# Division of attention by its sums: transposes and VectorE against factors sent through DRAM, with other places for the router's steps and for half of the last norms

## The chip, the cores and the metric

The kernel runs on one core of one Trainium2 chip, in one launch. The metric is the device time of that core in microseconds (us). Most of it is the span that the profile covers; the small rest lies around the span.

## The reference, cut to what matters

Two layers run over x of 8 x 256 tokens with 256 features. The first layer is an attention by correlation and a mixture of eight experts with balanced assignment; its output is added to x. The second layer is an ordinary cross attention with 16 heads of 16 features, and a mixture with one shared and eight routed experts, two of them for each token. The change is in the second layer:

```python
def _L1_xattn_ref(x, data, Wq, bq, Wkv, bkv, Wp, bp):
    q = (x @ Wq + bq).reshape(bs, n_ctx, HEADS, d)
    kv = (data @ Wkv + bkv).reshape(bs, n_data, HEADS, 2 * d)
    k, v = (kv[..., :d], kv[..., d:])
    scores = jnp.einsum('bqhd,bkhd->bhqk', q, k) * scale
    attn = jax.nn.softmax(scores, axis=-1)
    out = jnp.einsum('bhqk,bkhd->bqhd', attn, v).reshape(bs, n_ctx, WIDTH)
    return out @ Wp + bp

def _L1_ffn_ref(hidden_states, gate_W, w1_e, w3_e, w2_e, w1_s, w3_s, w2_s):
    probs = jax.nn.softmax(flat @ gate_W.T, axis=-1)
    top_v, top_i = jax.lax.top_k(probs, 2)
    # gates: top_v at top_i, zero elsewhere
    # routed: sum over e of gates * (silu(x w1_e) * (x w3_e)) w2_e
    # shared: mean over n of (silu(x w1_s) * (x w3_s)) w2_s
    return 0.5 * shared + 0.5 * routed

x = x + _L1_xattn_ref(_layernorm(x), ctx_1024, ...)
x = x + _L1_ffn_ref(_layernorm(x), ...)
```

The softmax of the attention is computed as exponentials, products with the values, and a division by the sum of the exponentials at the end. That division is what the change is about.

## The kernel before, in words

All work is in float32. The order of instructions on each engine is the order of the program's text: the scheduler is set to manual. The tokens of x lie in X, 128 per row of the tile, 16 such rows; a batch b is two of them (TPB = 2, S = 256).

**The attention loop.** Before it, keys KT and values VA of all batches are there, but for two last pieces of VA (`vals`). VA has 32 columns per head (HW): 16 features, and a column of ones that makes the product of exponentials and values carry the sum of the exponentials as its row 16 (DH). The loop runs over b = 0 to 7 and over c = 0, 1, a half of the heads, so 16 half batches. For each, `scores(b, c, kt)` is called with kt = 0 and 1, for each half of the keys: four matmuls (32 rows by 512 columns, L2652; the trace records each as two), each into its own PSUM buffer of ps_s (four buffers of 512 floats per partition), and four exponentials on ScalarE (L2660). Between and after the two calls stand pieces of other work: `values(prev, 0)` and `values(prev, 1)` of the half batch before (L2667), `keep` (L2677), which copies the product pv from its single PSUM buffer to ov, `queries` (L2619 and its copies QM at L2626 on ScalarE and L2633 on VectorE), `turn_q` (transposes of the normalised x for the queries, L2605), `add_y` (the first layer's output is added, loaded as yg from DRAM) and `batch_stats` for batches to come.

**The division.** For a batch whose two half batches are kept, `turn_back` transposes ov with eight matmuls against the identity (L2687), so that tokens are on the partitions; then VectorE takes reciprocals of the 16 sums (L2694) and multiplies (L2695) into `on`. `turn_out` transposes `on` back with four matmuls (L2706), VectorE copies to oT (L2712), and `project_out` multiplies by wp (L2718) and adds to X (L2726).

**The router and the mixture's rows.** `batch_stats(b, "m")` and `norm_m(b)` give the normalised rows HP; both halves of `norm_m` run on GpSimd (L2581). `turn_m` transposes them into HT (L2605, copy L2608 on ScalarE). `route(g)` is a generator of eight steps for four token rows, i.e. two batches: logits (L2797), a transpose (L2808), softmax and top two on VectorE, a cumulative count (L2850, L2851), and row numbers `to`. Each finished router puts eight sends in a list; `send(n)` issues the next n: indirect DMAs from GpSimd that write rows of HP to the table Td in DRAM (L2892). Each send waits for the one before it to land.

**After the loop.** The last values and norms, the routers 2 and 3 and the remaining sends are interleaved with `classic_up`, the shared expert's up projection for the first 512 tokens (L3196, eight steps, two PSUM buffers of ps_s for each); `first_down` is its down projection (L3439). Then come ten further blocks of 512 rows with a Strassen scheme (L3234, L3293). The first block of routed rows reads Td (R, L3491) and transposes R (L3509). The weights of the shared expert are loaded in five DMAs at the end of the half batch (0, 0).

**Queues.** Direct DMAs are issued from SP in program order, and an issue that waits holds all behind it.

The loop's centre:

```python
scores(b, c, 0)
if prev:
    values(*prev, 0)
send()
...          # c == 0: project_out(b - 2); c == 1: turn_back(b - 1), turn_m(b - 2)
scores(b, c, 1)
...          # c == 0: batch_stats(b - 2, "m"), norm_m(b - 2)
send()
if prev:
    values(*prev, 1)
    keep(*prev)
...          # c == 0: queries(b + 1, ...); c == 1: turn_out(b - 1), turn_q(b + 2)
```

Of the kernel before, what the change touches and what calls it, by code (L numbers as in the profile page):

```python
# [9 lines left out]
F32 = mybir.dt.float32  # L10
# [9 lines left out]
P = 128  # L20
# [1066 lines left out]
def fast_path(  # L1087
# [170 lines left out]
    B32 = p0.tile([P, 32], F32, name="B32")  # L1258
    miss = p0.tile([P, 2], F32, name="miss")
# [1270 lines left out]
    ps_s = banks.enter_context(tc.tile_pool(name="ps_s", bufs=4, space=PSUM))  # L2530
# [47 lines left out]
    def batch_norm(b, tag, dst, engs):  # L2578
        mv, r1 = norms.pop((tag, b))
        for j, eng in enumerate(engs):  # L2580
            eng.tensor_scalar(  # L2581
                dst[:, j, :],
                X[:, TPB * b + j, :],
                mv[:, j, 0:1],
                r1[:, j : j + 1],
                ALU.subtract,
                ALU.mult,
            )
# [54 lines left out]
    ex, pvs, ovs, ons, oTs = {}, {}, {}, {}, {}  # L2643

    def scores(b, c, kt):
# [3 lines left out]
        ps = [ps_s.tile([P, 2, S], F32, tag="p", name=f"p{g}") for g in range(4)]  # L2649
        for g in range(4):  # L2650
            rows = slice(32 * g, 32 * g + 32)
            nc.tensor.matmul(  # L2652
                ps[g].rearrange("p m q -> p (m q)"),
                KT[rows, c, k0 : k0 + P],
                QM[b][rows, c].rearrange("p m q -> p (m q)"),
                start=True,
                stop=True,
            )
        for g in range(4):
            nc.scalar.activation(e4[:, g], ps[g], AF.Exp, scale=scale)  # L2660
# [13 lines left out]

    def keep(b, c):
        ovs[b, c] = pxs.tile([P, 2, S], F32, tag="ov", name="ov", bufs=3)
        nc.vector.tensor_copy(ovs[b, c], pvs.pop((b, c)))  # L2677

    def turn_back(b):

        on = pxs.tile([P, TPB, NB, 2, 4, DH], F32, tag="on", name="on")
        ons[b] = on
        for qt in range(TPB):
            pt = ps_m.tile([P, NB, 2, 4, HW], F32, tag="pm", name="pt")
            for c in range(NB):
                for m in range(2):
                    nc.tensor.transpose(  # L2687
                        pt[:, c, m].rearrange("p g w -> p (g w)"),
                        ovs[b, c][:, m, qt * P : (qt + 1) * P],
                        ident,  # L2690
                    )
            pv = pt.rearrange("p c m g w -> p (c m g) w")
            rs = small.tile([P, H, 1], F32, tag="rs", name="rs")
            nc.vector.reciprocal(rs, pv[:, :, DH : DH + 1])  # L2694
            nc.vector.tensor_tensor(  # L2695
                on[:, qt].rearrange("p c m g d -> p (c m g) d"),
                pv[:, :, 0:DH],
                rs.to_broadcast([P, H, DH]),
                ALU.mult,
            )  # L2700

    def turn_out(b):
        pt = ps_m.tile([P, NB, TPB, P], F32, tag="pm", name="pt")
        for c in range(NB):
            for qt in range(TPB):
                nc.tensor.transpose(  # L2706
                    pt[:, c, qt, :],
                    ons[b][:, qt, c].rearrange("p m g d -> p (m g d)"),
                    ident,
                )  # L2710
        oTs[b] = pxs.tile([P, NB, TPB, P], F32, tag="oT", name="oT")
        nc.vector.tensor_copy(oTs[b], pt)  # L2712

    def project_out(b):
        pp = ps_m.tile([P, TPB, D], F32, tag="pm", name="pp")
        for qt in range(TPB):
            for c in range(NB):
                nc.tensor.matmul(  # L2718
                    pp[:, qt, :],
                    oTs[b][:, c, qt, :],  # L2720
# [10 lines left out]
    def norm_m(b):  # L2731
        batch_norm(b, "m", HP[:, TPB * b : TPB * (b + 1), 0:D], (nc.gpsimd,) * TPB)
# [169 lines left out]

    def load_up(pool, e):
# [60 lines left out]
    gates = None  # L2964
    prev = None
    for b in range(B):
        for c in range(NB):
            scores(b, c, 0)
            if (b, c) == (3, 0):
                router_weights()  # L2970
            if prev:
                values(*prev, 0)
            send()
            if gates:
                next(gates, None)
            if prev is None:
                list(vals(4, 1, ps_m, nc.vector.tensor_copy))
            elif b == 0:
                turn_q(1)
                norm_q(2, nc.vector, nc.vector)  # L2980
                queries(1, 0)
                queries(1, 1)
            elif c == 0:
                if b >= 2:
                    project_out(b - 2)
            else:
                if b >= 1:
                    turn_back(b - 1)
                if b >= 2:
                    turn_m(b - 2)  # L2990
                if 2 < b + 2 < B:
                    norm_q(b + 2, nc.vector, nc.vector if b < 2 else nc.gpsimd)
                    add_bias(b + 2)
            scores(b, c, 1)
            if gates:
                next(gates, None)
            if c == 0 and b >= 2:
                batch_stats(b - 2, "m")
                norm_m(b - 2)
            send()  # L3000
            if prev:
                values(*prev, 1)
                keep(*prev)
            if gates:
                next(gates, None)
            if c == 0:
                if 0 < b and b + 1 < B:
                    queries(b + 1, 0)
                    queries(b + 1, 1)
                if b + 2 < B and b:  # L3010
                    add_y(b + 2)
                    batch_stats(b + 2, "q")
                if b >= 4 and b % 2 == 0:
                    gates = route(b // 2 - 2)
                    next(gates)
            else:
                if b >= 1:
                    turn_out(b - 1)
                else:
                    add_bias(2)  # L3020
                if b + 2 < B:
                    turn_q(b + 2)
            if prev is None:
# [27 lines left out]
                WS = load_l1(wsp, -1)  # L3051
            if (b, c) == (1, 0):
                router_columns()
            prev = b, c
# [129 lines left out]
    def classic_up(wab, xs, acts):  # L3184

        for k in range(NK):
            act = act_tile()
            acts.append(act)
            for h in range(2):
                f = h * NK + k  # L3190
                fs = slice(f * P, (f + 1) * P)
                pgt = ps_s.tile([P, TB], F32, tag="p", name="pgt")
                pu = ps_s.tile([P, TB], F32, tag="p", name="pu")
                for m, ps in enumerate((pgt, pu)):
                    for kc in range(KC):
                        nc.tensor.matmul(  # L3196
                            ps,
# [7 lines left out]
                nc.scalar.activation(a, two(pgt), AF.Silu)  # L3205
                nc.vector.tensor_tensor(a, a, two(pu), ALU.mult)
# [245 lines left out]
    def first_down(wc, acts, between):  # L3452

        pys = [ps_s.tile([P, D], F32, tag="p", name="py") for _ in range(FULL)]

        for q in (0, 1):
            whole_down(pys[q], wc, acts, q, range(NK - 1))
        between()
        for q in range(FULL):
            whole_down(pys[q], wc, acts, q, range(NK - 1, NK) if q < 2 else range(NK))  # L3460
            add_whole(pys[q], q)
            if q % 2:
                nc.sync.dma_start(out=odv[:, q - 1 : q + 1, :], in_=X[:, q - 1 : q + 1, :])
# [208 lines left out]
    def run_all(*gens):  # L3672
        for gen in gens:
            for _ in gen:
                pass


    values(*prev, 0)
    project_out(B - 2)
    values(*prev, 1)  # L3680
    keep(*prev)
# [228 lines left out]
```

## Time and profile before

| | us |
|---|---|
| median of three runs | 831.42 (829.79 to 832.22) |
| the profiled execution, whole | 830.43 |
| its span | 828.7 |
| TensorE busy in the span | 806.3 |
| first score matmul of the attention loop | 223.0 |
| first matmul of the shared expert's down projection (L3439) | 381.1 |
| GpSimd's last send (L2892) starts | 427.1 |
| SP issues R (L3491) | 429.7 |
| first transposes of R (L3509) | 452.5 |

Times in the lower rows count from the start of the span. Granted TensorE clock: 0.998 of full. Durations of matmuls overlap: the profile gives a matmul the time from its start to its modelled end, while the next has begun. So the cost of a piece of TensorE work is read from the start of it to the start of what follows.

### The profile page before, as it was taken

What the parts mean: (1) busy time and instruction counts of PE and PEld (TensorE: products, weight loads), DVE (VectorE), ACT (ScalarE), POOL (GpSimd) and SP (SyncE); (2) the same over time, 40 slices, a digit from 0 to 9 for tenths busy, and PEclk for the clock granted to TensorE, in tenths of its full rate; (3) what the DMA queues carried; (4) which work ended last, traced back from release to release, by engine and by line L of the source; (5) the groups of instructions that cost most, each with busy time, mean ns of one, the idle gap of its engine ahead of it and who ended that gap; (6) DMA issues with size and microseconds to landing.
All of it is one profiled execution on the core that took longest, in us unless ns stands there. A gap on an engine that the chain in (4) does not pass through costs nothing.

```text
span 828.7 us, 13872 instructions
## 1 busy us (share of the span) xinstructions
PE 806.3 (97%) x5188; PEld 636.2 (77%) x5188; DVE 522.3 (63%) x1470; ACT 348.7 (42%) x720; POOL 216.8 (26%) x293
## 2 busy tenths in 40 slices
PE   7999999999999999999999999999999999999997
PEld 6546787778745555557898989797979798999996
DVE  6377877440456586555775866767676758586731
ACT  4344454324377777431333233333333433443430
POOL 6251131230125455452330000202111232112020
PEclk9999999999999999999999999999999999999999
DMA  8395567942160000042120474656575754311023
GB/s 261 97 277 177 178 207 224 297 158 84 51 178 15 14 1 28 34 168 89 67 67 26 142 242 135 190 168 187 172 199 161 201 167 122 105 13 20 8 35 124
DMA packets 87316, 105.40 MB, mean 127 GB/s; under 512 B 9000, under 2 KB 77832, under 8 KB 87208
## 3 DMA queue, kind: packets, MB, share of 16 engines
q1 hardware_dynamic: 78568, 91.10, 35.0%
q0 software_dynamic: 7920, 13.02, 7.2%
q8 instruction: 43, 0.70, 0.4%
q10 hardware_dynamic: 752, 0.30, 0.1%
q14 instruction: 33, 0.27, 0.1%
HBM read 80.61 MB, written 25.37 MB: 128 GB/s over the span
## 4 chain that ended last, share of the span: by engine, by line
PE 88%; DMA 5%; DVE 3%; POOL 2%; ACT 1%; issue 1%; ACTq 0%; SPq 0%; DVEq 0%; POOLq 0%
PE a L3234 18%; PE e L3234 9%; PE a L3293 9%; PE py L2389 6%; PE ph L2372 5%; PE B L3234 5%; PE e L3293 4%; PE p L2652 4%; PE py L3439 3%; PE pv L2667 3%; PE B L3293 2%; PE pp L2718 2%; DMA R<-NMd,ids 2%; PE pgt L3196 2%; PE pp L2619 2%; PE pu L3196 2%
## 5 line engine op out<-in xcount | busy, mean ns | idle before, releaser
L3518 POOL DMA_INDIRECT Od<-Y,ids x32 | 51.6, 1612 | 300.5 <-DVE T L3083 184.0
L3222 ACT COPY B<-a 128x512 f32<-128x512 f32 (+1 forms) x54 | 28.6, 531 | 180.5 <-PE a L3234 142.6
L2660 ACT ACTIVATE ex<-p,scale 128x512 f32<-128x512 f32 x128 | 77.2, 689 | 27.5 <-PE p L2652 26.3
L3234 PE MATMUL a<-T,HP 128*128 128x256 f32 x288 | 73.9, 379 | 0.0
L3083 DVE TENSOR_TENSOR cc<-e,s 128x512 f32<-128x512 f32 x44 | 30.4, 691 | 58.0 <-PE e L3234 58.0
L3234 PE MATMUL a<-RT,wab 128*128 128x256 f32 x256 | 66.6, 383 | 0.0
L3083 DVE TENSOR_TENSOR act<-act 128x256 f32<-128x256 f32 (+1 forms) x120 | 61.4, 512 | 2.7
L2372 PE MATMUL ph<-RT,w 128*128 128x256 f32 x256 | 61.7, 389 | 0.8 <-ACT RT L2359 0.7
L2389 PE MATMUL py<-w,A 128*128 128x256 f32 x256 | 61.6, 388 | 0.0
L3234 PEld LDWEIGHTS a<-T,HP 128*128 128x128 f32 x288 | 54.0, 190 | 7.0
L3234 PEld LDWEIGHTS a<-RT,wab 128*128 128x128 f32 x256 | 46.4, 190 | 8.4 <-issue 1.6
L2381 ACT ACTIVATE A<-ph,b1c 128x256 f32<-128x256 f32 x64 | 30.0, 472 | 53.9 <-PE ph L2372 50.6
L2372 PEld LDWEIGHTS ph<-RT,w 128*128 128x128 f32 x256 | 45.3, 190 | 8.9 <-ACT A L2381 1.1
L2389 PEld LDWEIGHTS py<-w,A 128*128 128x128 f32 x256 | 46.6, 190 | 6.4
L2892 POOL DMA_INDIRECT Td<-HP,to x32 | 32.9, 1030 | 56.9 <-DMA Td<-HP,to 51.6
L2652 PE MATMUL p<-QM,KT 32*128 32x512 f32 x256 | 43.4, 640 | 0.4 <-DVE QM L2633 0.4
L3083 DVE TENSOR_TENSOR act<-act,cc 128x512 f32<-128x512 f32 x44 | 30.4, 691 | 17.6 <-ACT act L3268 17.1
L2399 POOL DMA_INDIRECT Yd<-Y,ids x16 | 15.7, 984 | 81.9 <-DVE Y L2398 49.0
L2667 PE MATMUL pv<-ex,VA 128*32 128x256 f32 x512 | 34.5, 385 | 0.2 <-DVE ov L2677 0.2
L3249 ACT COPY s<-a 128x512 f32<-128x512 f32 x44 | 25.7, 585 | 20.4 <-PE a L3234 20.4
L2667 PEld LDWEIGHTS pv<-ex,VA 128*32 128x32 f32 x512 | 13.5, 109 | 27.0 <-issue 11.7
L3234 PE MATMUL e<-T,wab 128*128 128x256 f32 x128 | 33.0, 380 | 0.3 <-DVE T L3083 0.3
(525 smaller groups left out, 1745.0 us busy)
## 6 DMA issues: line engine op xcount, KB each, us to landing
w<-in_L_ffn_w_dram SPq DMA_DIRECT2D x16, 1024.0 KB, 6.0
wab<-in_L_ffn_w_e_dram SPq DMA_DIRECT2D x16, 1024.0 KB, 4.9
wc<-in_L_ffn_w_e_dram SPq DMA_DIRECT2D x8, 1024.0 KB, 5.4
sab<-in_L_ffn_w_e_dram SPq DMA_DIRECT2D x32, 256.0 KB, 2.9
R<-Td SPq DMA_DIRECT2D x8, 530.0 KB, 3.7
sc<-in_L_ffn_w_e_dram SPq DMA_DIRECT2D x16, 256.0 KB, 2.8
Td<-blank SPq DMA_DIRECT2D x2, 1590.0 KB, 10.2
X<-in_x_dram SPq DMA_DIRECT2D x4, 512.0 KB, 5.3
```

Source lines behind the costliest of these rows:

```text
L2372: nc.tensor.matmul(ph, w1[:, kc, f * P : (f + 1) * P], RT[:, kc, :], start=(kc == 0), stop=(kc == KC - 1),)
L2381: nc.scalar.activation(A[:, f, :], ph, AF.Gelu_apprx_tanh, bias=b1c[:, e, f : f + 1])
L2389: nc.tensor.matmul(py, A[:, f, r * P : (r + 1) * P], w2[:, f, :], start=(f == 0), stop=(f == NF - 1),)
L2652: nc.tensor.matmul(ps[g].rearrange("p m q -> p (m q)"), KT[rows, c, k0 : k0 + P], QM[b][rows, c].rearrange("p m q -> p (m q)"), start=True ...
L2660: nc.scalar.activation(e4[:, g], ps[g], AF.Exp, scale=scale)
L2667: nc.tensor.matmul(pvs[b, c][32 * g : 32 * g + 32, m, :], VA[:, b * TPB + kt, 8 * c + 2 * g + m, :], ex[b, c, kt][:, g, m, :], start=(kt = ...
L2892: nc.gpsimd.indirect_dma_start(out=Td, out_offset=bass.IndirectOffsetOnAxis(ap=to[g][:, k, j : j + 1], axis=0), in_=HP[:, GT * g + j, :], ...
L3083: eng.tensor_tensor(out, a, b, op)
L3196: nc.tensor.matmul(ps, wab[:, m, kc, fs], xs[kc], start=(kc == 0), stop=(kc == KC - 1),)
L3234: nc.tensor.matmul(ps[:, m * HT2 : (m + 1) * HT2], self.w.get(m, left, self.k), self.x.part[right], start=start and m == 0, stop=True, ski ...
L3293: nc.tensor.matmul(ps[:, qs], self.acts[k][:, left, qs], self.w.get(right, k), start=start and i == 0 and k == 0, stop=(k == NK - 1), skip ...
L3518: nc.gpsimd.indirect_dma_start(out=Od, out_offset=bass.IndirectOffsetOnAxis(ap=ids, axis=0), in_=Y, in_offset=None, compute_op=ALU.add,)
```

## The change

In `scores`, ps_s has two buffers of 1024 floats in place of four of 512, two of the four matmuls write to each, and an exponential covers one such buffer. `turn_back` and `turn_out` are gone. `keep` now sends the sums from ov to a tile rs of 128 x 16 and ov itself to DRAM (VD). `factors`, one half batch later, takes reciprocals of rs on VectorE, writes them to DRAM (FD), loads the 16 feature rows of each head from VD (num) and each head's factors from FD, repeated over 16 partitions (fac). `scaled_values`, another half batch later, multiplies both on GpSimd into oT. In the loop, both halves of `values` and `keep` stand between the two calls of `scores`; `queries` and `turn_m` (of b - 3 in place of b - 2) follow the second call at c = 0, `turn_q` and `project_out` at c = 1. `norm_m` has one row on GpSimd and one on VectorE, apart in time. Routers 0 and 1 start at (4, 1) and (6, 1) in place of (4, 0) and (6, 0), and their steps stand at other places. The shared weights come in six DMAs, one per half batch. After the loop, the same pieces stand in another order; the sends of routers 1 and 2 that are left wait for router 2 to finish. `classic_up` and `first_down` use the larger PSUM buffers, and `first_down` adds and stores its results in pairs.

```diff
-    ps_s = banks.enter_context(tc.tile_pool(name="ps_s", bufs=4, space=PSUM))
+    ps_s = banks.enter_context(tc.tile_pool(name="ps_s", bufs=2, space=PSUM))
...
-        ps = [ps_s.tile([P, 2, S], F32, tag="p", name=f"p{g}") for g in range(4)]
+        ps = [ps_s.tile([P, 2, 2, S], F32, tag="p", name=f"p{j}") for j in range(2)]
...
-        for g in range(4):
-            nc.scalar.activation(e4[:, g], ps[g], AF.Exp, scale=scale)
+        for j in range(2):
+            nc.scalar.activation(
+                e4[:, 2 * j : 2 * j + 2], ps[j], AF.Exp, scale=scale
+            )
...
     def keep(b, c):
-        ovs[b, c] = pxs.tile([P, 2, S], F32, tag="ov", name="ov", bufs=3)
-        nc.vector.tensor_copy(ovs[b, c], pvs.pop((b, c)))
-
-    def turn_back(b):
...
-    def turn_out(b):
...
+        ov = pxs.tile([P, 2, S], F32, tag="ov", name="ov")
+        nc.vector.tensor_copy(ov, pvs.pop((b, c)))
+        rs = pxs.tile([P, 16], F32, tag="rs", name="rs")
+        nc.sync.dma_start(
+            out=rs, in_=ov[DH::32].rearrange("g m (y e) -> g (m y) e", e=16)
+        )
+        VD = dram.tile([P, 2, S], F32, name=f"VD{b}_{c}")
+        nc.sync.dma_start(out=VD, in_=ov)
+        parts[b, c] = VD, rs
+
+    def factors(b, c):
+        VD, rs = parts[b, c]
+        rr = pxs.tile([P, 16], F32, tag="rr", name="rr")
+        nc.vector.reciprocal(rr, rs)
+        FD = dram.tile([4, 2, S], F32, name=f"FD{b}_{c}")
+        nc.sync.dma_start(
+            out=FD.rearrange("g m (y e) -> (g m y) e", e=16), in_=rr
+        )
+        num = pxs.tile([P, S], F32, tag="num", name="num")
+        fac = pxs.tile([P, S], F32, tag="fac", name="fac")
+        half = [slice(m * P // 2, (m + 1) * P // 2) for m in range(2)]
+        for m in range(2):
+            nc.sync.dma_start(
+                out=num[half[m]],
+                in_=VD.rearrange("(g w) m q -> g w m q", g=4)[:, 0:DH, m],
+            )
+        for m in range(2):
+            nc.sync.dma_start(
+                out=fac[half[m]],
+                in_=FD[:, m].unsqueeze(1).to_broadcast([4, DH, S]),
+            )
+        parts[b, c] = num, fac
+
+    def scaled_values(b, c):
+        num, fac = parts.pop((b, c))
+        if c == 0:
+            oTs[b] = pxs.tile([P, NB, S], F32, tag="oT", name="oT")
+        nc.gpsimd.tensor_tensor(oTs[b][:, c, :], num, fac, ALU.mult)
...
+            if c == 1 and b + 2 < B:
+                norm_q(b + 2, nc.vector, nc.vector if b < 2 else nc.gpsimd)
+                add_bias(b + 2)
+            if len(before) > 1:
+                factors(*before[-2])
+                next(shared_loads, None)
+            if before:
+                values(*before[-1], 0)
+                values(*before[-1], 1)
+                keep(*before[-1])
...
+            if c == 1 and b in (4, 6):
+                gate = route(b // 2 - 2)
+                next(gate)
+            if len(before) > 2:
+                scaled_values(*before[-3])
...
             scores(b, c, 1)
...
+            elif c == 0:
+                if b + 1 < B:
+                    queries(b + 1, 0)
+                    queries(b + 1, 1)
+                if b >= 3:
+                    turn_m(b - 3)
+            else:
+                if b + 2 < B:
+                    turn_q(b + 2)
...
+                if b >= 2:
+                    project_out(b - 2)
+                    batch_stats(b - 2, "m")
+                    norm_m(b - 2, nc.gpsimd)
...
+                if b >= 2:
+                    norm_m(b - 2, None, nc.vector)
...
+    last = before[-1]
+    factors(*before[-2])
+    values(*last, 0)
+    values(*last, 1)
+    scaled_values(*before[-3])
+    keep(*last)
     project_out(B - 2)
...
+    factors(*last)
     acts0 = []
     up0 = classic_up(WS[0], [HT[:, kc, 0:TB] for kc in range(KC)], acts0)
     next(up0)
-    turn_back(B - 1)
-    gate2 = route(2)
-    next(gate2)
+    turn_m(B - 3)
+    scaled_values(*before[-2])
     next(up0)
-    turn_out(B - 1)
-    next(gate2)
+    gate = route(2)
+    next(gate)
+    turn_m(B - 2)
+    scaled_values(*last)
+    next(gate)
     next(up0)
     project_out(B - 1)
     batch_stats(B - 1, "m")
-    norm_m(B - 1)
-    next(gate2)
-    turn_m(B - 2)
+    norm_m(B - 1, nc.gpsimd)
+    next(gate)
+    next(gate)
+    norm_m(B - 1, None, nc.vector)
+    next(gate)
     next(up0)
-    next(gate2)
-    next(gate2)
+    run_all(gate)
+    send(len(sends))
     next(up0)
-    run_all(gate2)
-    send(len(sends))
     turn_m(B - 1)
```

## The prediction

> **What bounds the kernel now.** I read the page's busy row and chain first, then TensorE's timeline over the attention stage, ScalarE's beside it, and the DMA table. The page names the engine:
>
> ```profile
> PE 806.3 (97%) x5188; PEld 636.2 (77%) x5188; DVE 522.3 (63%) x1470; ACT 348.7 (42%) x720; POOL 216.8 (26%) x293
> ...
> PE 88%; DMA 5%; DVE 3%; POOL 2%; ACT 1%; issue 1%; ACTq 0%; SPq 0%; DVEq 0%; POOLq 0%
> ```
>
> TensorE carries 88% of the chain, and in the changed stage (first score matmul at 223.0 us, first matmul of the shared expert's down projection, L3439, at 381.1 us) it shows almost no gap. So an instruction taken off TensorE here is time. But a busy row also hides stalls. The end of batch 7 in TensorE's timeline (start, duration, instruction):
>
> ```profile
> 334.69 1.07 PE L2667 MATMUL pv<-ex,VA 128*32 128x256 f32 x16
> 335.69 2.53 PE L2652 MATMUL p<-QM,KT 32*128 32x512 f32 x8
> 338.15 1.07 PE L2667 MATMUL pv<-ex,VA 128*32 128x256 f32 x16
> 339.16 1.09 PE L2687 MATMUL pt<-ident,ov 128*128 128x128 f32 x8
> 340.08 0.66 PE L2605 MATMUL pt<-ident,HP 128*128 128x128 f32 x4
> 340.67 1.14 PE L2652 MATMUL p<-QM,KT 32*128 32x512 f32 x8
> 341.74 1.07 PE L2667 MATMUL pv<-ex,VA 128*32 128x256 f32 x16
> 342.75 0.66 PE L2706 MATMUL pt<-ident,on 128*128 128x128 f32 x4
> 343.63 1.29 PE L2667 MATMUL pv<-ex,VA 128*32 128x256 f32 x16 [0.23 <-DVE ov L2677]
> ```
>
> Costs come from start to start: a score group takes 1.07 us (340.67 to 341.74), half of a value product 1.00, the transposes of L2687 0.92, those of L2706 0.5 (0.44 to 0.58 elsewhere). The group at 335.69 takes 2.46 us for the same eight matmuls. ScalarE's timeline says why:
>
> ```profile
> 327.02 2.42 ACT L2660 ACTIVATE ex<-p,scale 128x512 f32<-128x512 f32 x4 [0.47 <-PE p L2652]
> ...
> 334.63 4.73 ACT L2660 ACTIVATE ex<-p,scale 128x512 f32<-128x512 f32 x8 [2.53 <-PE p L2652]
> ```
>
> Four exponentials take 2.42 us, and only 1.0 to 3.0 us of other TensorE work lies between two score groups that use the same PSUM buffers. Where it is 1.0, TensorE waits inside the group. Going through the timeline, the excess over 1.07 us sums to 6.9 us (largest: 1.5 at 225.1, 1.0 at 237.0, 1.0 at 328.5, 1.4 at 335.7), and bracketed idle to 3.0.
>
> The same as a budget for 223.0 to 381.1: 32 score groups x 1.07 = 34.2; 32 value halves x 1.00 = 32.0; 14 query halves x 0.96 = 13.4; 8 output projections x 1.9 = 15.2; 15 turns of norms x 0.52 = 7.8; turn_back 8 x 0.92 = 7.4; turn_out 8 x 0.5 = 4.0; four routers x 0.8 = 3.3; two key/value products 2.1; the shared expert's up projection 8 x 3.44 = 27.5. Sum 147; elapsed 158.1; **about 11 us is waiting**.
>
> **What the Trainium skill says.** "Trainium Kernel Development and Optimization", section "Performance Expectations", calls matmul busy time a bad metric. The trace agrees: the 2.53 us group counts as busy. "DMA: Bandwidth & Descriptors", section "Anatomy of one DMA", puts the fixed part of a DMA at about 2.0 us, mostly the receipt of the write; section "Queues, rings and completion order" says that each DMA engine consumes descriptors in ring order, so a small transfer stands behind a large one. The trace agrees on the first (last column: us to landing) and shows no clean case of the second:
>
> ```profile
> yg<-Yd SPq DMA_DIRECT2D x8, 256.0 KB, 2.6
> wab_-1_6540<-in_L_ffn_w_s_dram SPq DMA_DIRECT2D x4, 512.0 KB, 5.2
> Od<-X SPq DMA_DIRECT2D x6, 256.0 KB, 2.1
> ids_s<-ids_p SPq DMA_DIRECT2D x4, 0.1 KB, 1.8
> ```
>
> "GPSIMD Engine Reference", section "4.1 Engine selection", has two-input elementwise work about twice as slow on GpSimd as on VectorE. Here 128x512 takes 1.27 us (L2597) against 0.68 (L2553).
>
> **The change part by part.**
>
> *TensorE loses turn_back and turn_out*: 8 x (0.92 + 0.5) = **11.4 us**, all in the bounding queue: on the path. Queries, projections, norm turns and expert matmuls keep their number.
>
> *Exponentials two PSUM buffers at a time.* In a run of four, each costs 0.58 us; a copy of 256 more elements costs 0.22 (L1428: 0.37 and 0.59), so 512 more cost 0.44 to 0.58 and a double one 1.02 to 1.16. I take 1.02: a set falls from 2.42 to about 2.1 us, ScalarE from 32 x 2.42 to 32 x 2.1, 10 us less. That is off the path except where TensorE waits for it. The price: the first matmuls of the next group now wait for a double exponential.
>
> *Both value halves together, projection and turns elsewhere.* Between score groups TensorE now always has 2.0 us (values) or 2.0 to 2.5 us (c=0: queries and turn_m; c=1: turn_q and projection). From the start of a group, its two exponentials end at 0.54 + 0.2 + 1.05 = 1.8 and 2.85 us; the next group needs the buffers at 1.07 + 2.0 = 3.07 and 3.6. So the scores stall goes, except at the start, where one key/value product gives only 1.07 us (0.3 lost). The 11 us of waiting could fall to nothing; I keep 4.5 (below).
>
> *What replaces the transposes.* Per half batch SP issues seven more DMAs (112 in all, 7 x 0.36 = 2.5 us of issue per step): rs and VD after keep; FD, two num, two fac in factors. VectorE loses 16 x (0.25 + 0.42) + 8 x 0.68 = 16.2 us, gains 16 reciprocals x 0.25 = 4 and 8 norms x 0.41 = 3.3: net -9. GpSimd loses 8 x 1.22 and gains 16 products between 0.64 (half of L2597) and 1.27; I take 0.64, so nothing; 1.27 is 10 us more, hidden since the product has a whole step before the projection reads it. The norm halves on VectorE wait for GpSimd's r1 (0.72 + 4 x 0.28 after the statistics): up to 2 us in which the next reciprocal and keep stand behind.
>
> The new waits make a cycle: a reciprocal waits for rs; FD waits on SP for the reciprocal, fac for FD's landing, and the next rs is issued behind fac. Its length: 0.25 + 2.1 (FD) + 0.72 (two fac issues) + 2.1 (rs with issue) = 5.2 us per step. The step on TensorE is half of 4 x 1.07 + 4 x 1.00 + 1.92 + 1.92 + 1.05 = 13.2, so 6.6. It fits. In the six steps with a 512 KB piece of the shared weights ahead of rs, rs may land with that piece, some 4.4 us: cycle 7.5. Steps of batch 1 have no projection yet (5.4 us each), so lateness builds from 0.3 towards 7 us at batch 3, while the reciprocal may be about 6.9 late before keep holds the next value product: I lose **2 us** at the most likely, 0 to 8 by bounds. Behind the waiting reciprocal on VectorE are keep, QM, hT and X adds; behind FD on SP the Y loads and shared weights; behind num/fac on GpSimd the norm chain and sends. A negative bound has no reason: a wait can't gain.
>
> *The end.* The last product: keep 0.7, rs 2.1, then the reciprocal behind batch 6's statistics and norm (to 6.7 us after the last values), FD 2.1, fac 0.7 + 2.2, product 0.64 to 1.27: 12.3 to 13. TensorE reaches that projection after 1.9 + 3 x 3.44 + 2 x 0.5 + 0.7 = 14. Covered by 1 to 2 us; I lose **1**, with **1.2** for router steps (lT's transposes) and the start's 0.3: 4.5 in all.
>
> *Sends.* 14 instead of 11 stand after the second-last router: 14 + 8 at 2.8 us from about 345 end near 407, R lands near 411; its transposes (now 452.5, then about 434) don't wait. Cover now: 429.7 + 3.7 = 433.4 against 452.5. Earlier loads, router_weights and the down projection's pairing: nothing; hidden under TensorE, same count.
>
> *Sum*: 11.4 + 11 - 4.5 = **18 us**. Profiled execution 830.43 (span 828.7 + 1.7), which is 1.0 below the median of 831.42: 812.4 for such an execution, **813.4** for the median.
>
> **Rivals.** (1) *The waits form again*, since buffers are handed over in coarser pieces and VectorE is held by reciprocals: only the transposes count, 820. For it: VectorE and ScalarE are at 60 to 80% in these stretches; against it: the 2 us of cover between groups. (2) *All waiting goes*: 831.4 - 22.4 = 809, less if the later stages tighten. (3) *The DMA cycle paces the loop*, slower. It decides from 6.6 + 22.5/15 = 8.1 us per step, where it has eaten the gain, so landings of 3.4 us where I took 2.1. With 4.0 each (landings of 8 us do occur for NMd behind other loads) a cycle is 9.4 with a weight piece: 15 x 2.8 = 42 us, less 22.4: 850. Against it: landings of 1.8 to 2.6 on quiet queues, and this stage moves little. (4) *No effect*, because routed rows come late: needs 20 us of slack lost; 831.
>
> **Chances.** Main case 0.60; rival 1 0.18; rival 2 0.09; rival 3 0.10; no effect 0.03. Under 0.3% (2.5 us) a measurement can't tell from none. Faster 0.87, same 0.03, slower 0.10. The range takes main case and rivals 1 and 2 with their bounds: 805 to 823.
>
> **What would show it.** Right: no line with ident,ov or ident,on; 64 exponentials of 128x1024 near 1.1 us; score groups at 1.1 us nearly throughout; the shared expert's down projection starting near 363 instead of 381.1; what follows it as long as before. Wrong: value products waiting for ov while VectorE's reciprocals wait for DMA rs, or steps above 7 us; ScalarE's double exponentials above 1.3 us; expert transposes waiting for R.

## The result and the profile after

The changed kernel takes **851.28 us** (849.18 to 853.4), against 831.77 for the kernel before on the same chip: ratio 1.0239 (1.0204 to 1.0275). The forecast was 813.4, with a range of 805 to 823. The profiled execution took 852.79 us, with a span of 851.1.

The page's busy row and the first line of its chain, for the changed kernel:

```profile
PE 800.2 (94%) x5092; PEld 630.2 (74%) x5092; DVE 512.3 (60%) x1454; ACT 338.1 (40%) x656; POOL 217.9 (26%) x301
...
PE 78%; DMA 10%; DVE 5%; issue 2%; POOL 2%; SPq 1%; ACT 1%; ACTq 0%; POOLq 0%; DVEq 0%
```

TensorE is 6 us less busy, but its share of the chain fell from 88 to 78%, and DMA's rose from 5 to 10%. The time sits in the changed stage, from the first score matmul to the first matmul of the shared expert's down projection (225.7 to 403.75): **178.1 us, against 158.1 before**. What follows takes 447.35 us (before 447.6). The first score matmul came at 223.0 before, at 225.7 after and between 222.4 and 225.7 in the other runs, so a single execution's total carries some 3 us that are not the change's. Stages are compared for that reason; each is from one profiled execution, and the same instructions can differ there too, as the step (4, 1) of two runs below shows by 2 us. Where the two disagree, the medians decide.

A step is the time from the first score group of a half batch (b, c) to that of the next. Nothing is lost up to the start of (2, 1): five steps sum to 32.7 us, against 36.3 before, where 3.3 us of transposes and a projection stood among them. Of the ten steps that follow, five take 10.7, 9.3, 8.5, 12.5 and 9.1. Three of the waits between 213 and 440 us of the changed kernel (columns: total, times, longest; `rr` is a reciprocal, `pp` a projection, `pv` a value product):

```profile
DVE rr L2701 <- DMA rs<-ov: 32.1, 11, 6.7
...
PE pp L2731 <- POOL oT L2725: 8.3, 1, 8.3
...
PE pv L2676 <- DVE ov L2689: 2.5, 3, 1.0
```

VectorE's reciprocals stand 32 us for rs; TensorE itself waits for the value copy `ov` for only 2.5. The rest of VectorE's lateness reaches TensorE through other instructions. The bracketed waits of TensorE's timeline in this stage sum to **29.0 us** (2.3 before). By releaser: VectorE 14.4 (router masks and copies 6.5 at the count and weight matmuls; h, the normalised x for the queries, and lT, the router's logits, 4.9; ov 2.5; other 0.5), GpSimd 13.3 (the product 8.3, normalised rows 5.0), ScalarE 1.2. With the 135.6 us of work that the budget left (147 less 11.4), 6.4 of waiting inside score groups and 6.9 of matmuls at half speed, that makes 177.9 of the 178.1. The same account of the kernel before (147, 6.9 and 2.3) leaves 1.9 of its 158.1 without a name, so the sum is good to about 2 us.

The chain of the changed kernel inside one such step (start, us, what):

```profile
261.83 5.74 DMA rs<-ov
267.66 0.26 DVE rr L2701
267.94 0.32 SPq L2703
268.37 0.53 SPq L2710
...
269.56 0.51 SPq L2715
...
270.68 0.45 SPq L2920
271.17 5.61 DMA rs<-ov
...
298.24 3.38 DMA rs<-ov
```

It is a closed loop of 9.3 us: rs lands after 5.7, reciprocal, FD, two num, two fac, a piece of the shared weights (L2920), the next rs. The sums are 8 KB. Six of these transfers were issued just behind a 512 KB piece: five landed in 5.2 to 5.9 us, the first in 4.0. Without one, where VectorE stood waiting, they took some 1.9 us (the first of all, at 238.03) and 3.1 to 4.3 (four, among them that at 298.24). The time from one rs to the next was 9.3 to 9.5 us in four steps, 6.9 to 8.8 in the others up to 314.5.

After the loop, TensorE's timeline of the changed kernel (start, duration; brackets: wait and releaser):

```profile
353.85 0.70 PE L2731 MATMUL pp<-wp,oT 128*128 128x256 f32 x2
362.88 2.93 PE L2731 MATMUL pp<-wp,oT 128*128 128x256 f32 x6 [8.33 <-POOL oT L2725]
365.60 4.57 PE L3229 MATMUL pgu<-HT,wab_s 128*128 128x512 f32 x8
370.44 3.60 PE L3229 MATMUL pgu<-HT,wab_s 128*128 128x512 f32 x8
...
386.85 0.19 PE L2863 MATMUL pc<-mk,ones_b 128*128 128x32 bf16 x1 [2.28 <-DVE mk L2859]
...
386.92 5.38 PE L3229 MATMUL pgu<-HT,wab_s 128*128 128x512 f32 x8
```

The projection of batch 6 waits 8.33 us, after two of its eight matmuls, for a product of 0.73 us. GpSimd's timeline of the same kernel says what the product stood behind:

```profile
356.44 1.01 POOL L2905 DMA_INDIRECT Td<-HP,to  x1 [2.64 <-DMA Td<-HP,to]
...
360.97 1.09 POOL L2905 DMA_INDIRECT Td<-HP,to  x1 [0.18 <-issue]
362.09 0.73 POOL L2725 TENSOR_TENSOR oT<-num,fac 128x256 f32<-128x256 f32 x1
```

Two sends, and between them the five small steps of a norm and one of its rows (1.36 us). And the up steps after the gaps take 4.57 and 5.38 us where 3.60 is usual: part of the same eight matmuls runs at half speed. The profile's granted TensorE clock says so too: 0.50 of full from 362.9 to 365.6 and 0.67 from 386.9 to 392.1, where 1.00 is usual.

### The profile page after: what moved, and what is told of

Read it like the earlier page. It is cut to its first block, busy times and chain, and to the rows that moved or that the text cites. A ratio compares the mean times of both kernels' runs of the same rounds, so it can differ in the third digit from the quotient of the medians.

```text
span 851.1 us, 13830 instructions
## 1 busy us (share of the span) xinstructions
PE 800.2 (94%) x5092; PEld 630.2 (74%) x5092; DVE 512.3 (60%) x1454; ACT 338.1 (40%) x656; POOL 217.9 (26%) x301
## 4 chain that ended last, share of the span: by engine, by line
PE 78%; DMA 10%; DVE 5%; issue 2%; POOL 2%; SPq 1%; ACT 1%; ACTq 0%; POOLq 0%; DVEq 0%
PE a L3267 18%; PE e L3267 9%; PE a L3326 8%; PE py L2394 6%; PE ph L2377 6%; PE B L3267 4%; PE e L3326 4%; DMA rs<-ov 4%; PE py L3472 3%; PE pgu L3229 3%; PE B L3326 2%; DMA R<-NMd,ids 2%; PE pp L1424 1%; PE pp L1403 1%; PE p L2659 1%
## 5 line engine op out<-in xcount | busy, mean ns | idle before, releaser
L3553 POOL DMA_INDIRECT Od<-Y,ids x32 | 51.5, 1608 | 297.2 <-DVE T L3117 178.1
L2667 ACT ACTIVATE ex<-p,scale 128x1024 f32<-128x1024 f32 x64 | 67.8, 1111 | 44.4 <-PE p L2659 44.4
L2676 PE MATMUL pv<-ex,VA 128*32 128x256 f32 x512 | 32.4, 396 | 2.5 <-DVE ov L2689 2.5
L2676 PEld LDWEIGHTS pv<-ex,VA 128*32 128x32 f32 x512 | 15.4, 113 | 23.7 <-issue 7.6
```

The lines of the kernel that those rows point to most:

```text
L2667: nc.scalar.activation(e4[:, 2 * j : 2 * j + 2], ps[j], AF.Exp, scale=scale)
L2676: nc.tensor.matmul(pvs[b, c][32 * g : 32 * g + 32, m, :], VA[:, b * TPB + kt, 8 * c + 2 * g + m, :], ex[b, c, kt][:, g, m, :], start=(kt = ...
L3553: nc.gpsimd.indirect_dma_start(out=Od, out_offset=bass.IndirectOffsetOnAxis(ap=ids, axis=0), in_=Y, in_offset=None, compute_op=ALU.add,)
```

## Experiments

The theories. **A**: the DMA cycle with a piece of weights ahead of rs. **B**: GpSimd's queue, where products and norms stand behind sends. **C**: the double score buffers. **N**: the new order itself, where TensorE comes too early to small steps of the router. Ratios are to the kernel before on the same chip, with 95% intervals.

| run | us | ratio | stage |
|---|---|---|---|
| the change | 851.28 | 1.0239 (1.0204 to 1.0275) | 178.1 |
| weights_behind_rs | 842.18 | 1.0143 (1.0108 to 1.0178) | 169.9 |
| constant_sums | 3563.31 | 4.2875 (4.2753 to 4.2997) | 170.8 |
| products_on_dve | 848.97 | 1.0210 (1.0175 to 1.0245) | 175.3 |
| factors_after_keep | 840.85 | 1.0117 (1.0080 to 1.0154) | 168.7 |
| fac_after_and_dve | 842.9 | 1.0142 (1.0108 to 1.0176) | 168.2 |
| fac_dve_fewer_sends | 836.46 | 1.0064 (1.0046 to 1.0082) | 165.0 |
| mended | 833.98 | 1.0033 (1.0017 to 1.0050) | 163.1 |
| products_later | 831.57 | 1.0000 (0.9981 to 1.0018) | 161.4 |
| tail_later | 827.15 | 0.9932 (0.9911 to 0.9954) | 153.3 |
| transposes_new_order | 838.9 | 1.0099 (1.0062 to 1.0137) | 162.6 |
| transposes_mended | 833.2 | 1.0020 (1.0004 to 1.0036) | 160.6 |
| before_pairs | 830.17 | 0.9985 (0.9973 to 0.9998) | 156.8 |
| filled_gaps | 854.54 | 1.0279 (1.0258 to 1.0300) | 180.6 |

**weights_behind_rs** issues the piece of weights behind rs and VD:

```diff
                 factors(*before[-2])
-                next(shared_loads, None)
             if before:
...
                 keep(*before[-1])
+                if len(before) > 1:
+                    next(shared_loads, None)
```

> The changed kernel with each 512 KB piece of the shared weights issued after rs and VD of the half batch, not before them. Theory A (the cycle reciprocal, FD, fac, weight piece, rs paces the half batches, because rs lands 5.2 to 5.9 us after its issue behind a weight piece): rs lands in 3 to 3.5 us, the steps between (2,1) and (5,0), 9.3 us in the changed kernel, come to 7 to 7.5 us, and the kernel gains 8 to 12 us. Theory B (GpSimd's queue, in which the products stand behind sends, paces the loop): no change before (5,1), so under 2 us. Theory C (the double exponentials and two PSUM buffers): no change.

Measured: 9 us less, 8.2 of them in the stage, as theory A said. The step of 10.7 became 7.4. Its chain:

```profile
257.34 3.60 DMA rs<-ov
261.31 2.97 DMA FD<-rr
265.41 3.40 DMA rs<-ov
```

rs now lands in 3.0 to 3.8 us; FD takes its place behind the piece and needs 2.9 to 3.2, where in the changed kernel fac was issued 1.6 us after FD. The cycle is 7.2 to 8.1 us. So the place of one line was worth nearly half of the loss, and the cycle is still longer than a step.

**constant_sums** has the reciprocals read a tile of ones, with no rs at all. It leaves the division out; the values that come of it send the later routed experts through the kernel's general path, so that the total of 3563 us says nothing and only the stage can be read.

```diff
-        rs = pxs.tile([P, 16], F32, tag="rs", name="rs")
-        nc.sync.dma_start(
-            out=rs, in_=ov[DH::32].rearrange("g m (y e) -> g (m y) e", e=16)
-        )
+        rs = ones[:, 0:16]
```

> The changed kernel without the DMA rs: the reciprocals read a tile of ones that is there from the start, so the division by the sums is left out; all other DMAs stay. Theory A: no reciprocal waits, the cycle is open, the steps fall to TensorE's 6.6 us until the sends begin, and 15 to 25 us go; what then remains over 813 is the sends' and the clock's part. Theory B: only 0 to 4 us go, since the products still stand behind sends. Theory C: no change.

Measured: 7.2 us less in the stage, between the two theories' ranges and no more than moving the piece brings. With every wait for rs gone, 12.7 us of the 20 are still lost: the DMA cycle is not the only cause.

**products_on_dve** puts the products on VectorE:

```diff
-        nc.gpsimd.tensor_tensor(oTs[b][:, c, :], num, fac, ALU.mult)
+        nc.vector.tensor_tensor(oTs[b][:, c, :], num, fac, ALU.mult)
```

> The changed kernel with scaled_values on VectorE in place of GpSimd. Theory B: the projection of batch 6, which waited 8.3 us for a product that stood behind sends, no longer waits, and the steps from (5,1) on (7.5 us) come nearer to 6.6: 8 to 14 us go. Theory A: VectorE now also waits for fac, which is later than rs, so the steps up to (5,0) stay at 9.3 us or grow; the end gains at most the 8 us of that wait, some of it lost again to VectorE's own waits: 0 to 6 us go, or some are added.

Measured: 2.7 us less in the stage, all at the end of it, within theory A's 0 to 6; the intervals of the two ratios overlap. The steps up to (5, 0) still hold those of 11.0, 9.6, 8.4 and 12.1. The tail's wait fell from 8.33 to 5.71 us. VectorE's timeline of this run says why not further:

```profile
357.83 0.41 DVE L2588 TENSOR_SCALAR HP<-X,b_mv,b_r 128x256 f32<-128x256 f32 x1 [4.44 <-POOL b_r L2580]
```

VectorE's row of a norm waits 4.44 us for GpSimd's part of that norm, which begins at 355.94, behind a send; the product follows at 358.32. So most of the rest is GpSimd's queue as well, at one remove.

**factors_after_keep** takes the reciprocals and all that follows behind the value copy of the same step, with the piece of weights:

```diff
-            if len(before) > 1:
-                factors(*before[-2])
-                next(shared_loads, None)
             if before:
...
                 keep(*before[-1])
+                if len(before) > 1:
+                    factors(*before[-2])
+                    next(shared_loads, None)
```

> The changed kernel with factors (and the weight piece) of a half batch put after keep, so that keep and rs of a step no longer stand behind the reciprocal, FD's landing and fac of the same step. Theory A: the cycle is cut, rs has a whole step to land, keep comes at once, value products don't wait for ov; the steps up to (5,0) fall to 6.6 to 7.2 us and the kernel gains 14 to 20 us, with theory B's part (products behind sends, 8 us at the end) left. Theory B: under 3 us. Theory C: no change.

Measured: 10.4 us less, between the two theories' ranges. No reciprocal waits any more, and four of the five steps from (2, 1) to (4, 1) take 6.8 to 6.9 us, as theory A said; (3, 1) takes 11.3. Yet the stage is only 1.2 us shorter than with the piece moved. The lateness went on to GpSimd, which now waits 21.5 us for fac, and TensorE waits 5.9 for a product, 3.5 for normalised rows behind sends, 2.3 and 2.2 for router masks.

**fac_after_and_dve** adds products_on_dve's edit to that.

> factors_after_keep (840.9 us) with scaled_values on VectorE as well, where it now stands behind keep and so behind most of fac's landing. Theory B, for what is left (in factors_after_keep GpSimd waited 21.5 us for fac and 39.5 us for sends' landings, with the norm chain and the products behind): GpSimd no longer waits for fac, batch 6's product (5.9 us of idle TensorE) no longer stands behind sends, and h at (3, 1) and the like come in time: 8 to 15 us go, to 826 to 833. Rival: VectorE, waiting for fac in place of GpSimd, holds QM and hT, and the time stays within 3 us of 840.9.

No gain, as the rival said: VectorE waits 13.0 us for fac instead of GpSimd. A product that stands ahead of its landing holds up the one engine as it did the other.

**fac_dve_fewer_sends** adds to that one line, so that no send stands in mid step at c = 1:

```diff
-            send()
+            if c == 0:
+                send()
```

> As fac_after_and_dve, and at c = 1 no send stands between the values and the norm chain of the same step; these sends go out at the end. Theory B: the norm chain of batches 4 and 5 (3.5 us of TensorE waiting for HP in factors_after_keep) no longer stands behind a landing, another 3 to 6 us go; the last send ends later, but the routed rows still have over 10 us to spare. Rival: the sends weren't what held the norm, under 2 us; or the routed rows now come late, and the kernel is slower.

3.2 us less in the stage, 6.4 in the medians. TensorE's wait for HP fell from 3.2 to 1.0: theory B holds for the norms, which shared GpSimd's queue with the sends. The step (4, 1), ahead of the first send and so with the same work in both runs, took 8.94 us in fac_after_and_dve and 10.95 here; that much is the execution's, not the edit's.

**mended** adds that the router's count matmuls stand further behind the vector work that feeds them (half a step in the loop, an up step in the tail).

> As fac_dve_fewer_sends, and the router's count matmuls (2.2 to 2.3 us of TensorE waiting for mk or for a PSUM buffer at (5, 0) and after the loop) stand further behind the steps that feed them: at (5, 1) and (7, 1), and one up-projection step later at the end. TensorE's waits of over 2 us, after each of which about 3.4 us ran at half clock, are then gone: 4 to 8 us less than fac_dve_fewer_sends, near 815 if all works. Rival: VectorE's own queue sets the end and nothing goes.

Another 2.5 us in the medians (1.9 in the stage), where 4 to 8 were forecast. The waits for router masks are gone, but that for batch 6's product grew from 4.4 to 6.5 us.

**transposes_new_order** has the order, score buffers and places of the changed kernel, with `turn_back` and `turn_out` in place of the division through DRAM.

> The changed kernel's order, exponentials and sends, but with the old division: turn_back and turn_out on TensorE and VectorE in place of keep's DMAs, factors and scaled_values. If theory A and B hold (the division through DRAM and its product on GpSimd cost the time), the DMA cycle and the products behind sends are gone and TensorE has its 11.4 us of transposes back: 816 to 828, below the kernel before, from the scores' waits that the new order removes. If the new order itself (norms and routers on other half batches) costs the time: 840 to 860.

It loses 1%, some 8 us, to the kernel before, although it does the same work. So of the change's 20 us some 8 come with the new order alone, and 12 with the division through DRAM in that order. Where the 8 lie, from TensorE's timeline:

```profile
304.62 0.18 PE L2862 MATMUL pc<-mk,ones_b 128*128 128x32 bf16 x1 [2.27 <-DVE QM L2640]
...
304.75 2.09 PE L2659 MATMUL p<-QM,KT 32*128 32x512 f32 x8
306.77 2.62 PE L2676 MATMUL pv<-ex,VA 128*32 128x256 f32 x32
```

A wait of 2.27 us for the router's mask, then a score group of 2.0 and a value product of 2.6 where 1.07 and 1.9 are usual. **transposes_mended** moves the router's counts and the sends there as in mended.

> The new order with the old division by transposes (838.9 us, stage 162.6), and beside it the router's count matmuls further behind the vector work that feeds them and no send in mid step at c = 1. Theory N (the new order's own loss lies in TensorE waiting for the routers' vector work, 2.3 us twice, and in the half clock that follows, 2 to 3 us twice): stage 155 to 157, time 831 to 834, so level with the kernel before. Rival (the loss lies in the order's uneven steps and in the coarser score buffers, which this doesn't touch): stage 161 or more, 837 or more.

833.2 us, in theory N's range: it holds for some 6 us of the order's loss. The stage of 160.6 missed its 155 to 157; it fell by 2.0 only, the profiled execution of transposes_new_order, 835.05, being its fastest. In this order and with these moves the two divisions are level: mended, with its reciprocals behind keep and its products on VectorE, has 833.98, and the intervals of the two ratios overlap. A wait of 2.94 us for the last projection's oT and 2.8 of slow matmuls behind it are left.

**before_pairs** is the kernel before with the double score buffers and exponentials alone.

> The kernel before, in its own order, with the score buffers and exponentials in pairs alone (ps_s two buffers of 1024, first_down and classic_up as in the change). Theory P (as the prediction: double exponentials of 1.1 us shorten a set from 2.42 to about 2.2 us, so the 6.9 us by which score groups exceed 1.07 fall to some 3 to 5): stage 154 to 156, time 827 to 830. Theory C (coarser hand-over forms waits where only 1 us of other work lies between two score groups): stage 160 to 164, time 833 to 838.

1.3 us less (interval 0.2 to 2.2), at the edge of theory P's range: theory C falls for the old order, and so does most of the gain forecast for the pairs. The excess of the 32 score groups over 1.07 us is 4.8 us, against 6.9. The new order wasn't tried without pairs.

**products_later** starts from mended: products another half batch later (three buffers of num and fac), `turn_m` after the value products at c = 1, the projection ahead of `turn_q`, the tail's projection of batch 6 behind two up steps.

```diff
-            if len(before) > 2:
-                scaled_values(*before[-3])
+            if len(before) > 3:
+                scaled_values(*before[-4])
```

> Starts from the run with the routers' steps moved (833.98 us, stage 163.1 us). Products on VectorE one more half batch later (three buffers of num and fac); both tail products of batch 6 and its projection behind two up steps of the shared expert; turn_m after the value products at c = 1; projection ahead of turn_q at c = 1. Theory A (the division through DRAM costs only where somebody stands behind a late landing; every such place of the earlier run is named and moved): of its listed waits go 6.5 + 0.7 and 2.9 of half clock at the tail projection, 1.9 + 0.7 and 0.9 of half clock at (3,1), 1.4 + 1.5 for HP, some 1 for h: about 17 us, less 2 for a bare end of (7,0). Stage 148 to 152, time 819 to 824. Rival D (eight DMAs per half batch are too many for SP's queue or VectorE: the waits only move): stage 159 or more, time 830 or more.

The loop's steps became short, as theory A said: from (2, 1) on, those of c = 0 take 6.4 us, those of c = 1 7.2 to 8.7. But (7, 0) had nothing left between two score groups, and the tail's product now stood behind the last reciprocal, so that the total gained only 2.4 and landed, with a stage of 161.4, in rival D's range. **tail_later** moves those:

```diff
+            if (b, c) == (B - 1, 0):
+                scaled_values(*before[-3])
...
+    turn_m(B - 4)
     values(*last, 0)
     values(*last, 1)
     keep(*last)
     scaled_values(*before[-4])
+    scaled_values(*before[-3])
...
     next(up0)
     factors(*last)
```

> Starts from the run with the products one half batch later (831.57 us, stage 161.4: the steps of the loop are as short as forecast, but the bare end of (7,0) costs 2.0 of waiting and 2.6 of half clock, and the tail 2.4 for a product that stands behind the last reciprocal, 3.8 for the router's mk, 1.0 for a norm, and 3 of half clock). Edit: the projection of batch 5 at the end of (7,0), turn_m of batch 4 at the end of (7,1); both products of batch 6 ahead of the last reciprocal; the projection of batch 7 one up step earlier, the rows of norm_m apart, turn_m of batch 6 one up step later. Theory A (each wait has its own place and goes with it): 1.2 of waiting stays at (7,1), the tail comes to about 36 us; stage 149 to 152, time 819 to 822. Rival D (the waits only move, since VectorE is full in the tail): stage 158 or more, 828 or more.

**827.15 us, 0.7% faster than the kernel before**, between theory A's 819 to 822 and the rival's 828; the stage of 153.3 is near theory A's 149 to 152. Moving a wait removes most of it, and a smaller one appears. From its timeline of TensorE, what is left:

```profile
329.85 1.99 PE L2731 MATMUL pp<-wp,oT 128*128 128x256 f32 x8 [1.89 <-DVE oT L2725]
...
355.19 2.54 PE L2731 MATMUL pp<-wp,oT 128*128 128x256 f32 x8 [2.01 <-DVE oT L2725]
...
357.74 4.66 PE L3234 MATMUL pgu<-HT,wab_s 128*128 128x512 f32 x8
```

Bracketed waits are 8.8 us (29.0 in the changed kernel), 7.2 of them for products.

**filled_gaps** puts unused matmuls into two of the changed kernel's gaps: 33 ahead of the projection of batch 6, 7 ahead of router 2's count.

> The changed kernel with 33 unused matmuls of 128x256 (0.23 us each, 7.6 us) ahead of the projection of batch 6 after the loop, where TensorE waits 8.33 us, and 7 more (1.6 us) ahead of the count of router 2, where it waits 2.28. Theory H (the matmuls after a gap are slow because TensorE has stood still): projection 1.9 in place of 2.93, the up step after it 3.6 in place of 4.57, the up step after the count 3.6 in place of 5.38; 3.8 us less in the stage, time 847.5 where the changed kernel has 851.3. Rival (they are slow for another reason, such as traffic of the weights or a shared limit that the wait only accompanies): the same three durations and 851.

```profile
354.11 14.51 PE L3710 MATMUL pf<-wp,ident 128*128 128x256 f32 x66
368.46 1.89 PE L2731 MATMUL pp<-wp,oT 128*128 128x256 f32 x8
370.19 3.60 PE L3229 MATMUL pgu<-HT,wab_s 128*128 128x512 f32 x8
...
391.11 3.68 PE L3229 MATMUL pgu<-HT,wab_s 128*128 128x512 f32 x8
```

The fill was mis-sized: a float32 matmul is recorded as two, so each took 0.44 us and the fill 14.5 where 7.6 was meant. That is why the total is 3 us longer. But the three durations in dispute are 1.89, 3.60 and 3.68, as theory H said, where they were 2.93 (for six matmuls, here eight), 4.57 and 5.38. The granted clock is 1.00 in both places. The weights' traffic is no rival: from 390 to 396 us DMA moves 394 GB/s here, at full speed, against 363 from 386.9 to 392.1 in the changed kernel. Behind the gap of 8.33 us the slow matmuls come from TensorE's standing still; for gaps near 2 us the last section says more.

## Why the prediction was wrong, by its own steps

**Right.** TensorE lost the transposes. A double exponential takes 1.11 us (1.02 taken, bounds 1.02 to 1.16), by the page's group of the changed kernel:

```profile
L2667 ACT ACTIVATE ex<-p,scale 128x1024 f32<-128x1024 f32 x64 | 67.8, 1111 | 44.4 <-PE p L2659 44.4
```

What follows the stage is as long as before. Routed rows come in time: the last send starts at 453.5, R is issued at 456.1, and its transposes stand at 475.5 without a wait. But the sends were to start near 345 and end near 407. The last 22 start only at 386.7 and come every 3.2 us; by R's 3.7 us to landing some 16 us of cover are left, where 434 less 411 made 23.

**The cycle was too short.** "0.25 + 2.1 (FD) + 0.72 (two fac issues) + 2.1 (rs with issue) = 5.2 us per step", 7.5 with a piece of weights. Measured: 9.3 to 9.5 in four of the six steps with a piece. rs lands there in 5.2 to 5.9 us where 4.4 was taken, an issue of num or fac takes 0.51 to 0.54 where 0.36 was taken, and four of them stand in the cycle, not two: num's issues also stand between the reciprocal and the next rs. FD's landing, which the sum had at 2.1, was hidden under them. The loss taken was "2 us (0 to 8 by bounds)"; factors_after_keep, which moves the piece too, gets back 9.4 of the stage. Queue order, which the prediction read in the Trainium skill ("DMA: Bandwidth & Descriptors", "Queues, rings and completion order") and for which the trace of before had no clean case, has one now: behind a 512 KB piece the same 8 KB took 5.2 to 5.9 us five times of six, and 3.0 to 3.8 once weights_behind_rs had moved the piece. The fixed 2.0 us per DMA that the prediction took from the same page is stated there for transfers issued by GpSimd; these are SP's, and of the rs whose landing shows only the first, at 1.9, came near it.

Rival 3 named this cycle at 9.4 us and came to 850 (its terms make 851), nearly the measured time. It was right that a cycle of DMAs paces the steps with a piece. Its 9.4 came from FD landing in 4.0 us and rs in 4.4; measured in those four steps were at most 1.6 and 5.6 to 5.9, with issues that it left out, so the agreement is luck. So is that of the total: it had all 15 steps that long and no other loss, and the runs give the cycle only half of the 20 us.

**"Hidden since the product has a whole step before the projection reads it"** failed. Its 0.64 to 1.27 us was right (0.73); its place in GpSimd's queue was not looked at, which after the loop holds two sends and a norm ahead of it: TensorE waited 8.3 us. The tail was taken as a loss of 1.

**The order's other waits were taken as 1.2.** Normalised rows from GpSimd cost 5.0 of bracketed wait, only 1.9 of it behind a send (at 344.77; the first send starts at 322.2), and router masks, h and lT some 11. In part VectorE was held by its reciprocals, in part the order alone does it, as transposes_new_order shows; how the 11 divide is not shown.

**"So the scores stall goes, except at the start"** failed too: 6.9 us became 6.4. The exponentials of a set were to end 1.8 and 2.85 us after the group's start. In the changed kernel's group at 242.73 the first starts 1.23 after it (0.74 taken) and the set ends at 3.35. The four matmuls of a group run side by side: they start within 0.02 us and end together some 1.1 us later. The trace of before had shown it: the first exponential of the group at 244.62 started at 245.78, 1.16 later. For the same reason the next group needs both buffers at once, at 3.0 and not at 3.07 and 3.6, so the second holds it for 0.4 us. Many groups wait 0.4 to 0.5 us, and three, with only a key/value product (228.04) or `turn_q` (238.80, 251.46) ahead of them, about 1.0. Even before, only 6.9 + 2.3 of the "11 us of waiting" were waits that the timeline names; the bracketed idle was 2.3, not 3.0.

**Half speed after gaps had no term**: 6.9 us, of which some 4 lie behind the two gaps that filled_gaps filled. The granted clock accounts for all of it: in the stage TensorE worked 14.9 us at half clock, which costs 7.4 at most.

Together: 29.0 + 6.4 + 6.9 = 42.3 us of waiting where 4.5 were left in the sum; the difference, 37.8, is what lies between 813.4 and 851.3. The term that failed is thus the 4.5 for waits, and the largest parts of it are those above. Open stays how much of the division through DRAM is lost with the best order: tail_later has 153.3 us in the stage, transposes_mended 160.6, but tail_later's order wasn't tried with transposes.

## What to carry to other kernels

When a chain through DRAM takes the place of work on the bounding engine, write down the whole loop that it closes, with each issue of its queue and whatever large transfer stands ahead of a small one in that queue; put large loads behind the small transfer that someone waits for. Give each handed-over result the engine queue and the distance that keep it from standing behind a slow neighbour; here a product that was early blocked VectorE as it had blocked GpSimd. When a stall is moved, look for the next late one before counting the gain: here only the sixth move gave a kernel that beats the one before.

## What the runs showed of the hardware

A gap on TensorE can cost more than itself. After waits of 2.07, 2.27, 2.28 and 8.33 us the next matmuls ran at half clock for 3.4 us or more, which cost 1.6 to 2.2 us each time. The Trainium skill ("TensorE: Matmul & The Clock Gate", "HAM oscillation — how this bites in real kernels") states the effect, with gaps above some 3.4 us as its condition; in these runs gaps of 2.1 to 2.3 us were enough, and the measurement decides. Not every such gap did it: in the changed kernel one of 2.18 us at 269.10 was followed by matmuls of the usual length, and so were 2.69 us at 347.56 and 2.28 us at 370.56 in transposes_new_order. The last one stands ahead of the same router count that cost the changed kernel 1.7 us.

The traces show where it falls. In the stage of the changed kernel the granted clock is 0.50 from 302.70, 316.35, 357.31 and 388.03 on, for 3.41, 3.41, 10.24 and 3.41 us. The starts lie 13.65, 40.96 and 30.72 us apart, whole multiples of 3.41. Four windows of that grid in the changed kernel (from and to; length, TensorE busy, instructions, granted clock, DMA share, GB/s):

```profile
265.15:268.56 3.41, 1.77 (x9) 1.00 0.47 148
268.56:271.97 3.41, 2.87 (x41) 1.00 0.21 54
...
312.94:316.35 3.41, 1.34 (x13) 1.00 0.24 85
316.35:319.77 3.42, 3.42 (x36) 0.50 0.25 74
```

The gap of 2.18 us is split at 268.56, and nothing follows; that of 2.07 us lies in one window, and the next has half the clock. In all ten traces with more than one such stretch in the stage the starts lie on such a grid; three more have one stretch, which sets it. Of the 596 windows at full clock in the stages of these 13 traces, 34 hold 1.85 us or more of idle TensorE, and each of the 34 is followed by half clock; of the 549 with less than 1.6 us one is, and of the 13 between two. So waits in one window add up (1.81 and 0.69 us ahead of 277.52 in factors_after_keep), and a gap near 2 us costs or not by where it falls in the grid. The one of the 549 is in products_later, with a wait of 0.80 us at 327.85 in a window of score matmuls, which use 32 of 128 rows; why is open.
